# Two transformer layers on one core: layer norms turned by VectorE and transfers, with a token's four chunks side by side

## The chip, the cores and the metric

The kernel runs on one core of a Trainium2 chip. Its engines work side by side and wait for one another through semaphores: TensorE (PE in the profile; PEld is its loading of the stationary operand), VectorE (DVE), ScalarE (ACT), GpSimd (POOL), and SyncE (SP), which issues all of the kernel's transfers between HBM and SBUF. TensorE multiplies a stationary operand (up to 128 x 128) with a moving operand streamed past it, both from SBUF, and writes to PSUM. The metric is the time on the device in microseconds; lower is better. The time of a kernel is the median of its runs; before the change 1811.73 us, of three runs between 1811.0 and 1814.87.

## The reference

Two layers on x of 2 batches x 1024 tokens x 512 features, all in fp32. Each layer norms x over the features and adds a causal attention of 16 heads and a gated feed-forward part, both computed from the same normed x. The first layer's hidden width is 2048, the second's 1408, with scales on gate, up and down.

```python
x = L0_attn_X
xn = _layernorm(x, axis=-1)
x = x + _L0_attn_ref(xn, Wq, Wk, Wv, Wo) + _L0_ffn_ref(xn, w_gate, w_up, w_down)
xn = _layernorm(x, axis=-1)
x = x + _L1_attn_ref(xn, Wq, Wk, Wv, Wo) + _L1_ffn_ref(xn, gate_w, up_w, down_w, gate_s, up_s, down_s)
return x
```

The norm is (x - mean) / sqrt(var + 1e-5). The attention rotates queries and keys by position, masks what lies ahead, takes a softmax over the keys and multiplies with the values and Wo. The feed-forward part is (silu(xn gate^T) * (xn up^T)) down^T.

## The kernel before

The work is cut into four phases, one per layer and batch: (layer 0, batch 0), (0, 1), (1, 0), (1, 1). A phase works on 1024 tokens: eight tiles of 128, or two halves of 512 (`tb`, `TB = 512`). A phase's attention goes in four groups of four heads, each group in four blocks of 256 queries, each block in one to four steps over keys; that makes 40 steps a phase. The softmax of a step runs on ScalarE, VectorE and POOL while TensorE is five steps ahead (`LAG = 5`) with scores.

**xnT.** All projections need the normed x with features on the partitions. It is held as two tiles, `xnT[ph, 0]` and `xnT[ph, 1]`, one per half of the tokens, each of 128 partitions x 4 chunks of features x 512 tokens. The buffers are single: the next phase's tiles take the places of this phase's. For the two halves together, products are formed in a scheme with seven products in place of eight (`class Unit`, line 710, with `first`, `second`, `third` and `fourth`). It also needs differences between the blocks of xnT: the three tiles `xs` (`ln_sums`, line 680) and a last one put in place of a part of `xnT[ph, 1]` (`ln_last_sum`, line 691), all by POOL. `first` reads `xnT[ph, 0]`, `second` reads two of xs, `third` reads `xnT[ph, 1]`, `fourth` the last of xs. `Hidden` units make the hidden layer, `QueriesKeys` units queries and keys; in both xnT and xs are the moving operand of 128 x 512 matmuls (`product`, line 760). `Values` units use xnT and xs as the stationary operand (its own `product`, line 992). Every fp32 matmul leaves two records of TensorE in the profile.

**The norm of a later phase.** Some 22 steps before a phase ends, each tile of the next phase's x is loaded (`load_raw`), and VectorE takes its mean and variance (`ln_stats`); `ln_factors` makes the scale and offset. At the phase's end, when its last unit has read xnT, each tile is loaded once more, scaled by ScalarE (`ln_scale`, line 661), turned by four TensorE transposes of 128 x 128 into a PSUM bank, and copied into xnT by ScalarE (`ln_transpose`, line 668); with the second half come the sums. The products of the last hidden pair with the down weights (`d` in the profile) are done between these tiles. Then `QueriesKeys` of the new phase follows. The first phase has its own form (`ln_pair`, `transpose_pair`).

**What sets the order.** The kernel doesn't emit its instructions as it makes them. `Schedule.record` (line 237) keeps every operation with its dependencies and a cost from a table (`cost`); `emit` and `again` then place all of them on a simulated clock, engine by engine, by the time when they are due for TensorE, and issue them in that order (the call is line 278, so nearly every row of the profile shows that line; rows are told apart by their tiles). SP's queue takes transfers in this order, one after the other, each with its own wait. `class Fill` (line 1416) decides what TensorE does between attention steps: its `main` list holds units and hand-over work in order, `downs` and `outs` hold products that may be pulled forward when the head of `main` would have to wait (`needs` names what an item waits for). `queue_phase` (line 1552) fills these lists for a phase, the hand-over to the next one included.

Of the kernel before, what the change touches and what calls it, by code (L numbers as in the profile page):

```python
# [18 lines left out]
P = 128  # L19
# [3 lines left out]
TB = 512  # L23
# [7 lines left out]
NSQ = QB // SQ  # L31
EPS = 1e-5
# [122 lines left out]
class Schedule:  # L155
# [31 lines left out]
    def cost(self, eng, method, args, kwargs, outs, ins):  # L187
# [6 lines left out]
        if eng is self.tensor:  # L194
            if method == "transpose":
                mode, t = "full", 131.0
            else:
                lhs, rhs = args[1], args[2]
                small_k, small_m = lhs.shape[0] < P, lhs.shape[1] < P
# [306 lines left out]
def two_layers(ctx: ExitStack, tc: tile.TileContext, x_in, attn_w, ffn_w, ffn_s, rope, out):  # L506
# [126 lines left out]
    def transpose_pair(pair):  # L633

        tb, h = divmod(pair, 2)
        if h == 0:
            xnT[0, tb] = xp.tile([P, DC, TB], F32, tag=f"xnT{tb}", name=f"xnT0_{tb}")
        xn = normed.pop((0, pair))
        for n in range(2):
# [3 lines left out]
            (nc.vector.tensor_copy if n else nc.scalar.copy)(xnT[0, tb][:, :, ts(2 * h + n, P)], tr[:, 0])  # L643
# [17 lines left out]
    def ln_scale(ph, t):  # L661
        tb, q = divmod(t, 4)
        rstd, off = stats[ph, tb]
        s = raw_x.pop((ph, t))
        nc.scalar.activation(s, s, AF.Identity, bias=off[:, q : q + 1], scale=rstd[:, q : q + 1])
        normed[ph, t] = s

    def ln_transpose(ph, t):
        tb, q = divmod(t, 4)
        if q == 0:  # L670
            xnT[ph, tb] = xp.tile([P, DC, TB], F32, tag=f"xnT{tb}", name=f"xnT{ph}_{tb}")
        s = normed.pop((ph, t))
        tr = bank(f"tr{ph}_{t}", (P, DC, P))
        for c in range(DC):
            nc.tensor.transpose(tr[:, c, :], s[:, ts(c, P)], ident)
        nc.scalar.copy(xnT[ph, tb][:, :, ts(q, P)], tr)
        if tb == 1:
            ln_sums(ph, q)

    def ln_sums(ph, q):  # L680

        if q == 0:
            xs[ph] = [xp.tile([P, 2, TB], F32, tag=f"xs{n}", name=f"xs{n}_{ph}") for n in (1, 2, 4)]
        t1, t2, t4 = (t[:, :, ts(q, P)] for t in xs[ph])
        b11, b21 = (xnT[ph, 0][:, 2 * c : 2 * c + 2, ts(q, P)] for c in range(2))
        b12, b22 = (xnT[ph, 1][:, 2 * c : 2 * c + 2, ts(q, P)] for c in range(2))
# [4 lines left out]
    def ln_last_sum(ph):  # L691

        for c in range(2):
            b12, b22 = xnT[ph, 1][:, c, :], xnT[ph, 1][:, 2 + c, :]
# [15 lines left out]
    class Unit:  # L710
# [49 lines left out]
        def product(self, bank, a, b, start=False):  # L760
            for c in range(2):
# [3 lines left out]
                    b[:, c, :],  # L765
# [14 lines left out]
        def needs(self, kind):  # L780

            if kind == "second":
# [7 lines left out]
        def first(self):  # L790
# [4 lines left out]
            self.product(self.x, a11, x0[:, 0:2], start=True)  # L795
            one = self.one = keep(self.x, f"p1{self.name}")
            z = bank(f"uz{self.name}")
            self.product(z, a12, x0[:, 2:4], start=True)
# [18 lines left out]
        def third(self, nxt):  # L817
            (_, _, s3, _), _, s4 = self.blocks()
            x1 = xnT[self.ph, 1]
            self.product(self.x, s3, x1[:, 0:2])  # L820
# [3 lines left out]
            self.product(self.y, s4, x1[:, 2:4])  # L824
# [59 lines left out]
    def project_qk(which, tokens):  # L884
# [4 lines left out]
        for c in range(DC):  # L889
            nc.tensor.matmul(  # L890
                ps, wqk[0, 0, which][:, c, :], xnT[0, half][:, c, at : at + n], start=(c == 0), stop=(c == DC - 1)
# [921 lines left out]
```

## Time and profile before

| | |
|---|---|
| median of three runs | 1811.73 us |
| profiled execution, its time | 1814.8 us |
| its span, first to last instruction | 1812.9 us |
| mean granted clock of TensorE | 0.998 |
| PE busy | 1798.0 us, 99% |
| DVE busy | 1476.3 us, 81% |
| POOL busy | 1232.6 us, 68% |
| ACT busy | 1041.7 us, 57% |
| moved by transfers | 165.15 MB, 91 GB/s on average |
| transposes of later phases (tr<-ident,xr) | 96 |
| copies from PSUM into xnT | 28 by ACT, 584 ns each; 4 by DVE, 684 ns each |

Times in a row are microseconds unless marked ns. A row of a group reads: line, engine, operation, written tile <- read tiles, shapes, how many | busy time in all, mean ns of one | idle time of the engine just before them, and what ended it. In a timeline a row reads: start, length, engine, line, operation, how many. Matmuls are pipelined: a record is longer than the distance to the next one's start, so what a matmul costs is read from start to start.

### The profile page before, as it was taken

The page shows a single profiled execution, that of the slowest core. Times are in us where ns is not written, and L with a number is a line of the kernel's source. Part 1 is how long each engine was busy: PE and PEld are TensorE (multiplying, and loading weights), DVE is VectorE, ACT ScalarE, POOL GpSimd, SP SyncE. Part 2 cuts the span into 40 slices and gives each one's busy share as a digit, 9 for nine tenths or more (in the row PEclk, how much of TensorE's full clock was granted, in tenths as well). Part 3 has the DMA queues.
Part 4 walks back from the last instruction along what each step waited for, and adds up shares of the span by engine and source line. Part 5 has one row for each costly group of instructions (what it writes and reads, how often), then busy time and mean ns, then how long its engine had stood idle before and what let it go on. Part 6 is the DMA issues. An engine that isn't in the chain of part 4 may idle for free.

```text
span 1812.9 us, 25807 instructions
## 1 busy us (share of the span) xinstructions
PE 1798.0 (99%) x9406; PEld 880.0 (49%) x9406; DVE 1476.3 (81%) x1975; ACT 1041.7 (57%) x1240; POOL 1232.6 (68%) x1145
## 2 busy tenths in 40 slices
PE   9999999999999999999999999999999999999998
PEld 5464444444444644444444455444444464444443
DVE  3665988868879668779697798888979998989988
ACT  2444665556546565554575556576565757565762
POOL 6726875956868337446377894886779775866775
PEclk9999999999999999999999999999999999999999
DMA  5324343222232422222133324222223322221211
GB/s 192 99 82 137 114 148 120 67 80 82 80 113 88 138 72 68 70 82 89 56 97 102 115 76 160 76 80 71 77 84 98 125 69 71 70 69 50 67 39 71
DMA packets 140334, 165.15 MB, mean 91 GB/s; under 512 B 13360, under 2 KB 93488, under 8 KB 140208
## 3 DMA queue, kind: packets, MB, share of 16 engines
q1 hardware_dynamic: 140208, 163.50, 28.5%
q8 instruction: 75, 1.23, 0.3%
q14 instruction: 51, 0.42, 0.1%
HBM read 134.62 MB, written 28.84 MB: 90 GB/s over the span
## 4 chain that ended last, share of the span: by engine, by line
PE 89%; POOL 5%; DVE 3%; issue 1%; ACT 1%; DMA 1%; SPq 0%; POOLq 0%; ACTq 0%; DVEq 0%
PE d L278 24%; PE ux L278 19%; PE uy L278 9%; PE sc L278 8%; PE av L278 7%; PE ux_qk L278 5%; PE uz L278 5%; POOL acc L278 2%; PE uy_qk L278 2%; PE ux_v L278 2%; PE uz_qk L278 1%; PE uy_v L278 1%; DVE s L278 1%; PE ps_o L278 1%; PE tr L278 1%
## 5 line engine op out<-in xcount | busy, mean ns | idle before, releaser
L278 POOL TENSOR_TENSOR acc<-acc,s 128x512 f32<-128x512 f32 (+1 forms) x378 | 487.4, 1311 | 84.4 <-ACT s L278 79.9
L278 DVE TENSOR_TENSOR s<-s,mb 128x512 f32<-128x512 f32 (+1 forms) x384 | 489.6, 1300 | 12.5 <-DMA mb<-md 12.5
L278 DVE TRANSPOSE_TENSOR_REDUCE rmax<-s 128x32 f32<-128x1024 f32 (+1 forms) x320 | 351.5, 1117 | 63.9 <-POOL s L278 41.3
L278 PE MATMUL d<-wd,hT 128*128 128x512 f32 x864 | 400.1, 593 | 0.0
L278 ACT ACTIVATE s<-s 128x1024 f32<-128x1024 f32 (+1 forms) x320 | 304.9, 970 | 163.0 <-DVE s L278 161.0
L278 ACT ACTIVATE s<-sc 128x1024 f32<-128x1024 f32 (+1 forms) x320 | 283.3, 934 | 195.1 <-PE sc L278 184.0
L278 POOL TENSOR_TENSOR acc<-s 128x512 f32<-128x512 f32 (+1 forms) x128 | 169.2, 1328 | 195.3 <-ACT s L278 191.5
L278 PEld LDWEIGHTS d<-wd,hT 128*128 128x128 f32 x864 | 161.9, 190 | 192.6 <-issue 186.9
L278 ACT ACT_TABLE_LOAD x167 | 214.3, 1283 | 7.7 <-DVE s L278 4.7
L278 DVE TENSOR_TENSOR x<-d,x 128x512 f32<-128x512 f32 x224 | 151.3, 676 | 75.8 <-PE d L278 75.0
L278 PE MATMUL av<-s,v 128*32 128x256 f32 (+1 forms) x2560 | 159.2, 364 | 0.7 <-ACT s L278 0.5
L278 POOL TENSOR_SCALAR_AFFINE_SELECT s<-s 128x512 f32<-128x512 f32 x128 | 98.9, 784 | 67.0 <-ACT s L278 65.0
L278 PEld LDWEIGHTS av<-s,v 128*32 128x32 f32 x2560 | 67.6, 109 | 145.7 <-issue 97.2
L278 POOL TENSOR_TENSOR hT<-p,hT 128x512 f32<-128x512 f32 x53 | 72.5, 1367 | 77.9 <-ACT hT L278 77.9
L278 PE MATMUL d<-wo,oT 128*128 128x512 f32 x198 | 103.0, 602 | 1.2 <-DVE hT L278 1.2
L278 PE MATMUL ux<-xs,ws 128*128 128x512 f32 x212 | 101.7, 602 | 0.6 <-ACT p L278 0.6
L278 PE MATMUL ux<-xnT,wu 128*128 128x512 f32 x212 | 101.8, 602 | 0.1
L278 PE MATMUL ux<-xnT,wg 128*128 128x512 f32 x212 | 100.9, 598 | 0.4 <-DVE hT L278 0.4
L278 PE MATMUL ux<-xs,wu 128*128 128x512 f32 x212 | 101.2, 600 | 0.0
L278 PE MATMUL uy<-xs,ws 128*128 128x512 f32 x212 | 99.7, 593 | 0.3 <-DVE hT L278 0.3
L278 PE MATMUL uy<-xnT,ws 128*128 128x512 f32 x212 | 99.8, 593 | 0.0
L278 PE MATMUL uz<-xnT,wg 128*128 128x512 f32 x212 | 99.7, 593 | 0.0
(179 smaller groups left out, 2511.2 us busy)
## 6 DMA issues: line engine op xcount, KB each, us to landing
mb<-md SPq DMA_DIRECT2D x64, 512.0 KB, 3.8
wg<-in_gate SPq DMA_DIRECT2D x54, 256.0 KB, 2.9
wd<-in_down SPq DMA_DIRECT2D x32, 256.0 KB, 2.9
xr<-xm SPq DMA_DIRECT2D x32, 256.0 KB, 2.7
wu<-in_up SPq DMA_DIRECT2D x28, 256.0 KB, 3.0
s12gu<-ws SPq DMA_DIRECT2D x26, 256.0 KB, 2.0
ws<-s12gu SPq DMA_DIRECT2D x26, 256.0 KB, 2.6
wd<-wds SPq DMA_DIRECT2D x22, 256.0 KB, 2.9
```

What stands on the lines that cost most here:

```text
L278: target(*[get(a) for a in args], **{k: get(a) for k, a in kwargs.items()})
```

## The change

In the three later phases TensorE no longer transposes. Earlier in the phase before, when the factors are there, each tile is loaded again and scaled by ScalarE, and VectorE turns it in blocks of 32 x 32 into a tile `turned_x` in which a token's four feature chunks lie side by side. Four transfers per tile write it to HBM, which puts the blocks of a chunk on their partitions (runs of 512 bytes). When the last unit of the phase has read an old half of xnT, four transfers read the new half in (2 KB for each partition and tile). POOL makes all the sums after both halves are there. Statistics and scaling start some steps earlier, and `first` is told to wait for `xnT[ph, 0]`.

The layout of xnT and xs changes everywhere, the first phase included: from chunk x token to token x chunk. A chunk's tokens are then 16 bytes apart in xnT and 8 bytes apart in xs, where they were adjacent. All matmuls that read them, POOL's sums, and the first phase's copies out of PSUM follow.

```diff
     def transpose_pair(pair):
...
-            xnT[0, tb] = xp.tile([P, DC, TB], F32, tag=f"xnT{tb}", name=f"xnT0_{tb}")
+            xnT[0, tb] = xp.tile([P, TB, DC], F32, tag=f"xnT{tb}", name=f"xnT0_{tb}")
...
-            (nc.vector.tensor_copy if n else nc.scalar.copy)(xnT[0, tb][:, :, ts(2 * h + n, P)], tr[:, 0])
+            (nc.vector.tensor_copy if n else nc.scalar.copy)(
+                xnT[0, tb][:, ts(2 * h + n, P)], tr[:, 0].rearrange("p c t -> p t c")
+            )
...
     def ln_scale(ph, t):
...
         nc.scalar.activation(s, s, AF.Identity, bias=off[:, q : q + 1], scale=rstd[:, q : q + 1])
-        normed[ph, t] = s
-
-    def ln_transpose(ph, t):
-        tb, q = divmod(t, 4)
+        turned_x = tmp.tile([P, QSQ, SQ, DC], F32, tag="swapped", name=f"xt{ph}_{t}")
+        nc.vector.transpose(turned_x.rearrange("p f s c -> p c f s"), s.rearrange("p (c f s) -> p c f s", f=QSQ, s=SQ))
+        to = normed[ph, t] = xd.tile([P, QSQ, P], F32, tag=f"xn{t}", name=f"xnd{ph}_{t}")
+        for a in range(QSQ):
+            nc.sync.dma_start(
+                out=to[:, a, :].rearrange("(f s) e -> s f e", s=SQ),
+                in_=turned_x[ts(a, SQ)].rearrange("p f s c -> p f (s c)"),
+            )
+
+    def ln_read(ph, tb):
+        xnT[ph, tb] = xp.tile([P, TB, DC], F32, tag=f"xnT{tb}", name=f"xnT{ph}_{tb}")
+        for q in range(4):
+            nc.sync.dma_start(
+                out=xnT[ph, tb][:, ts(q, P)].rearrange("p t c -> p (t c)"), in_=normed.pop((ph, 4 * tb + q)).rearrange("p a e -> p (a e)")
+            )
...
-        if q == 0:
-            xnT[ph, tb] = xp.tile([P, DC, TB], F32, tag=f"xnT{tb}", name=f"xnT{ph}_{tb}")
-        s = normed.pop((ph, t))
-        tr = bank(f"tr{ph}_{t}", (P, DC, P))
-        for c in range(DC):
-            nc.tensor.transpose(tr[:, c, :], s[:, ts(c, P)], ident)
-        nc.scalar.copy(xnT[ph, tb][:, :, ts(q, P)], tr)
-        if tb == 1:
-            ln_sums(ph, q)
...
+            xs[ph] = [xp.tile([P, TB, 2], F32, tag=f"xs{n}", name=f"xs{n}_{ph}") for n in (1, 2, 4)]
+        t1, t2, t4 = (t[:, ts(q, P)] for t in xs[ph])
+        b11, b21 = (xnT[ph, 0][:, ts(q, P), 2 * c : 2 * c + 2] for c in range(2))
+        b12, b22 = (xnT[ph, 1][:, ts(q, P), 2 * c : 2 * c + 2] for c in range(2))
...
         def product(self, bank, a, b, start=False):
...
-                    b[:, c, :],
+                    b[:, :, c],
...
         def needs(self, kind):
+            if kind == "first":
+                return [xnT[self.ph, 0]]
...
     class Values(Unit):
...
-                        b[:, c, ts(2 * self.pair + n, P)],
+                        b[:, ts(2 * self.pair + n, P), c],
...
     def queue_phase(ph):
...
-                fill.at(t0 + per_phase - 22 + t, lambda t=t: load_raw(nxt, t))
-                fill.at(t0 + per_phase - 21 + t, lambda t=t: ln_stats(nxt, t))
-            fill.at(t0 + per_phase - 12, lambda: ln_factors(nxt, range(2)))
+                fill.at(t0 + per_phase - 24 + t // 2, lambda t=t: load_raw(nxt, t))
+                fill.at(t0 + per_phase - 23 + t // 2, lambda t=t: ln_stats(nxt, t))
+            fill.at(t0 + per_phase - 19, lambda: ln_factors(nxt, range(2)))
+            for t in range(QC):
+                fill.at(t0 + per_phase - 19 + t, lambda t=t: load_raw(nxt, t))
+                fill.at(t0 + per_phase - 18 + t, lambda t=t: ln_scale(nxt, t))
...
-        fill.main.insert(len(fill.main) - 2, (0.0, lambda: (raw(0), raw(1)), "other", None, 0))
-        fill.main.insert(len(fill.main) - 1, (0.0, lambda: scale(0), "other", None, 0))
-        for t in range(QC):
-
-            def one(t=t):
-                ln_transpose(nxt, t)
-                raw(t + 2)
-                scale(t + 1)
-
-            fill.add(0.7, one, "other", lambda t=t: [normed[nxt, t]])
-            if t == 1:
-                fill.add(0.0, waits)
-        fill.add(0.0, lambda: (ln_last_sum(nxt), marks.append(nxt)))
+        fill.main.insert(len(fill.main) - 3, (0.0, lambda: ln_read(nxt, 0), "other", None, 0))
+        fill.main.insert(len(fill.main) - 1, (0.0, lambda: ln_read(nxt, 1), "other", None, 0))
+        fill.add(0.0, waits)
+
+        def sums():
+            for q in range(4):
+                ln_sums(nxt, q)
+            ln_last_sum(nxt)
+            marks.append(nxt)
+
+        fill.add(0.0, sums)
```

The matmuls of `first`, `third`, `project_qk` and `hidden` follow the new layout in the same way, and the schedule's cost table now takes all of a stationary operand's columns to tell a small matmul from a full one.

## The prediction

> **What bounds the kernel now.** I read the page first for the engines' shares, then the timeline of TensorE around the first hand-over between phases, then the groups of instructions by shape.
>
> ```profile
> span 1812.9 us, 25807 instructions
> ...
> PE 1798.0 (99%) x9406; PEld 880.0 (49%) x9406; DVE 1476.3 (81%) x1975; ACT 1041.7 (57%) x1240; POOL 1232.6 (68%) x1145
> ...
> PE   9999999999999999999999999999999999999998
> ...
> PE 89%; POOL 5%; DVE 3%; issue 1%; ACT 1%; DMA 1%; SPq 0%; POOLq 0%; ACTq 0%; DVEq 0%
> ```
>
> TensorE (PE) works in every slice and is 89% of the chain that ended last. No other engine is full. So an edit is worth what it takes from, or adds to, TensorE's own list of work, as long as the other engines keep up. The hand-over itself, in the timeline (start, length, instruction, how many):
>
> ```profile
> 458.02 0.66 PE L278 MATMUL tr<-ident,xr 128*128 128x128 f32 x4
> 458.51 1.88 PE L278 MATMUL d<-wd,hT 128*128 128x512 f32 x4
> ...
> 480.30 0.60 PE L278 MATMUL tr<-ident,xr 128*128 128x128 f32 x4
> 480.74 3.60 PE L278 MATMUL d<-wd,hT 128*128 128x512 f32 x8
> 484.18 0.60 PE L278 MATMUL tr<-ident,xr 128*128 128x128 f32 x4
> 484.61 1.88 PE L278 MATMUL ux_qk<-xnT,wq 128*128 128x512 f32 x4
> 486.33 1.88 PE L278 MATMUL uz_qk<-xnT,wq 128*128 128x512 f32 x4
> ```
>
> Read start to start: a group of four transposes costs 0.43 to 0.50 us, and four records of 512 columns cost 1.72 us (484.61 to 486.33). That is 0.43 us a record, 0.84 ns a column, and it is the same wherever I looked. Each fp32 matmul of the program leaves two records. There is no idle time at this hand-over, so the transposes cost only their own length.
>
> **The change, part by part.** The sum is made against the profiled execution: 1814.8 us, of which 1812.9 is the span and 1.9 lies around it. It is 3.1 us above the median of the runs, 1811.73.
>
> *Transposes removed.* The eight groups of the first hand-over take 3.68 us start to start (0.49, 0.95 for two, 0.50, 0.44, 0.43, 0.44, 0.43). Three hand-overs: **-11.0 us** of TensorE's time. ScalarE also loses 24 copies out of PSUM at 0.58 us each; at 57% busy that buys nothing.
>
> *The new layout under the matmuls.* This is the part that nobody's list of instructions shows. In the changed kernel a chunk of xnT is read with 16 bytes from one token to the next; before, tokens were adjacent. Counted in the changed kernel's own order of instructions: 568 matmuls of 512 columns stream xnT, and 16 of 256 columns. Times two records: 1136 and 32, or 1152 records of full length. The xs tiles are read with a step of 8 bytes in 408 more (816 records). No row before has TensorE reading with a step, so the cost is bounded. From below: nothing. From above, by the nearest row, VectorE reading fp32 from SBUF with a wide step:
>
> ```profile
> L278 DVE TRANSPOSE_TENSOR_REDUCE rmax<-s 128x32 f32<-128x1024 f32 x192 | 232.8, 1224 | 22.4 <-ACT s L278 21.8
> L278 DVE TRANSPOSE_TENSOR_REDUCE rmax<-s 128x24 f32<-128x768 f32 x128 | 118.7, 955 | 41.5 <-POOL s L278 41.3
> L278 DVE TENSOR_REDUCE m<-mtr 32x32 f32<-32x128 f32 x64 | 17.2, 269 | 18.6 <-PE mtr L278 17.9
> L278 DVE TENSOR_REDUCE m<-rmax 128x32 f32<-128x256 f32 x16 | 9.3, 580 | 0.3
> L278 DVE TENSOR_REDUCE m<-rmax 128x32 f32<-128x128 f32 x16 | 5.8, 360 | 0.3
> ```
>
> Adjacent elements: (1224 - 955) / 256 = 1.05 ns each. With a step of 64 bytes (m from rmax): (580 - 360) / 128 = 1.72 ns. A step in PSUM (m from mtr) costs nothing of the kind, 269 ns for 128. So a read that meets a new piece of SBUF at every element pays, and the price is 1.72 ns. The Trainium skill, page "SBUF — State Buffer", section "Door 1: The DMA port swizzle", speaks against the change: SBUF is read in lines of 16 bytes, and a line must be hit at least twice for full speed. With 16 bytes from token to token each line is hit once, with 8 bytes twice. (The same passage also calls a stride of four fp32 free, so it does not decide alone; no run so far shows TensorE under it.)
>
> What each gives: by the row in absolute time, 512 x 1.72 = 0.88 us a record, 1152 x 0.45 = +519 us. By the row's ratio, 1.72 / 1.05 = 1.64, 1152 x 0.43 x 0.64 = +317 us. By the rule, read as one line taking the time of two elements, twice 0.43, 1152 x 0.43 = **+495 us**. I take the last: it lies between the two readings of the row and close to the absolute one (2 x 0.84 = 1.68 ns against 1.72), which I trust more than the ratio because VectorE's and TensorE's own steps differ. For xs I take nothing, as two elements share a line.
>
> *Stationary reads.* For the values, xnT and xs are the stationary operand: 448 loads of 128 columns, beside streams of 256 columns that take 0.215 us each. A load's record is 190 ns. If the 256 of them that load from xnT double their 128 x 0.84 = 107 ns, they just reach the end of their cover: between 0 and 256 x 0.107 = 27 us; I take **+10**.
>
> *VectorE's transposes.* 24 of 128x512. The row of the existing block transpose is 445 ns for 256; with 256 more at 1.05 ns it is 0.71 us, with stepped writes at 1.72 up to 1.15 us. That is 17 to 28 us in all, spread over some 20 of a phase's 40 steps; VectorE was busy 45.2 of the 58 us before the hand-over. TensorE runs five steps behind the softmax that VectorE feeds, and that covers it: **0**; uncovered, it is the 17 to 28 us.
>
> *Transfers.* Per phase 32 writes and 8 reads join SP's queue, 120 in all, at about 0.32 us of queue each (the issues of md and xr take that): 38 us of SP in 1800, and 12.6 MB on top of 165. What is moved past SP's queue: a write waits for its transpose, and behind it stand the weights and the pair md, mb of the row maxima, for which VectorE's subtraction waits (12.5 us in the whole run now). A write late by 2 us makes a subtraction late by 2 us, within the same five steps: **0**, at most +20.
>
> *The new wait at the hand-over.* The first product of the new phase waits for four reads of xnT, the second for eight differences that POOL makes after all eight reads. Summing TensorE's own work in the new order, from the last read of the old second half: 17.5, 19.2 and 21.1 us until the new phase's first product, and 29.9, 31.6 and 27.6 us until its first use of xs. A 256 KB read lands in 2.7 us, four of them in about 6. Eight differences took 0.73 us each, 6 us; with half as much again for steps over 8 bytes (the Trainium skill, "GPSIMD Engine Reference", section "Performance pitfalls for Q7 kernels"; no row here has such a step) 9 us. 6 + 9 = 15 against 27.6 leaves some 12 us for POOL's other work in between: **0**. Without that cover, each late microsecond is one on the end. The last sums, two of 1.39 us per phase, are needed later still.
>
> *The first phase.* The eight copies into xnT now read PSUM with a step (m from mtr: no price) and write 16-byte pieces: **0**, at most +3. Statistics and scaling only move earlier.
>
> Sum: 1814.8 - 11.0 + 495 + 10 = 2308.8 in a profiled run; less 3.1, **2305 us**.
>
> **The rivals.**
>
> *The step is free for TensorE (the other side).* In the av groups four 32-column matmuls stream side by side: 16 records of 256 columns in 1.00 us, four times the words of one stream out of the same partitions. So SBUF can give TensorE a word per 0.21 ns; if one fp32 stream, which uses only one per 0.84 ns, can draw on that, nothing is lost. Against it: those are four streams, each on its own adjacent line. Then 1814.8 - 11.0 - 3.1 = 1800.7, with a little for the first phase about **1802 us**. The sign turns at 11.0 / 1152 = 9.5 ns a record, 2.2% of 0.43 us: below that the change gains, above it loses.
>
> *A part of the price.* If VectorE's ratio carries over, +317: **2128 us**; contention of the many lines with the other engines' reads alone could be anything from +10 up.
>
> *The step is free, but the hand-over is late.* POOL or a transfer overruns its 12 us of cover by more than 5 us at each of three places, which outweighs the 11: **1815 to 1835 us**. The cover speaks against it.
>
> *No change that can be measured:* gain and small losses meet, 1808 to 1815 us.
>
> **How the numbers follow.** Full doubling 0.42, free 0.33, part of the price 0.13, late hand-over 0.07, no change 0.05. Within 0.2%, 3.6 us, a measurement of this kernel can't tell from no change. So faster 0.33, same 0.05, slower 0.62. The likeliest case's own range is 2270 to 2335 us (the row's absolute price on top, a few ns less a record below). Since both signs hold much of the chance, the range reaches from 1798 to 2335: it leaves out a gain beyond the transposes, and a doubling that also takes the stationary loads or the xs tiles at full price, together about 0.1.
>
> **What would show it.** Doubling: four records of a product on xnT stand 3.4 us apart, start to start, those on xs still 1.72; PE stays at 99%, while the shares of VectorE, ScalarE and POOL fall by a fifth. Free: both stay at 1.72 and the transposes are simply gone. Late hand-over: idle time of PE before ux_qk, released by a DMA or by POOL's xs. I am wrong outright if TensorE buffers whole lines or reads each word twice from one line, so that the step never shows.

## The result

The changed kernel takes **2358.1 us** (median of four runs, 2356.9 to 2358.6), beside 1812.7 us for the kernel before (1811.0 to 1814.9). The ratio is **1.301 [1.299, 1.303]**: 545 us slower. The prediction was 2305 us, with a range up to 2335. Direction and mechanism are those of the likeliest case; the size is 53 us short, a tenth of the loss, and the time lies 23 us above the range. Each ratio further on is against runs of the kernel before that were made beside that experiment (medians from 1811.3 to 1811.8 us).

The profile page of the kernel after, with the span, the engines' busy time, the chain that ended last, and four groups (busy us, mean ns of one record):

```profile
span 2356.8 us, 25763 instructions
...
PE 2345.2 (100%) x9310; PEld 900.2 (38%) x9310; DVE 1439.0 (61%) x1996; ACT 1038.6 (44%) x1219; POOL 1195.0 (51%) x1146
...
PE 98%; DVE 1%; POOL 1%; DMA 0%; issue 0%; ACT 0%; SPq 0%; POOLq 0%; DVEq 0%; ACTq 0%
...
L279 PE MATMUL d<-wd,hT 128*128 128x512 f32 x864 | 399.9, 594 | 0.0
...
L279 PE MATMUL ux<-xnT,wu 128*128 128x512 f32 x212 | 201.0, 1082 | 0.0
...
L279 PE MATMUL ux<-xs,wu 128*128 128x512 f32 x212 | 106.4, 623 | 0.0
```

TensorE runs 96 records fewer (the transposes' own) and is busy 547 us longer. The other engines do about the same microseconds of work as before in a span that is 30% longer, so their shares fall by a quarter: VectorE from 81% to 61%, ScalarE from 57% to 44%, POOL from 68% to 51%. Products that never touch xnT (`d`) have the length they had. Those on xnT have nearly doubled, and those on xs are a little longer than `d`. The same groups in the kernel before (busy us, mean ns) show that all three were alike:

```profile
L278 PE MATMUL d<-wd,hT 128*128 128x512 f32 x864 | 400.1, 593 | 0.0
...
L278 PE MATMUL ux<-xnT,wu 128*128 128x512 f32 x212 | 101.8, 602 | 0.1
...
L278 PE MATMUL ux<-xs,wu 128*128 128x512 f32 x212 | 101.2, 600 | 0.0
```

The timeline of TensorE at a hand-over of the kernel after (start, length, instruction, how many):

```profile
636.90 3.70 PE L279 MATMUL d<-wd,hT 128*128 128x512 f32 x8
640.44 3.76 PE L279 MATMUL ux_qk<-xnT,wq 128*128 128x512 f32 x4
644.02 3.78 PE L279 MATMUL uz_qk<-xnT,wq 128*128 128x512 f32 x4
647.62 1.90 PE L279 MATMUL d<-wd,hT 128*128 128x512 f32 x4
...
656.76 1.96 PE L279 MATMUL ux_qk<-xs,ws_qk 128*128 128x512 f32 x4
658.56 1.96 PE L279 MATMUL uy_qk<-xs,ws_qk 128*128 128x512 f32 x4
660.36 1.88 PE L279 MATMUL d<-wd,hT 128*128 128x512 f32 x4
```

Start to start, four records on xnT take 3.58 to 3.60 us (640.44 to 644.02 to 647.62), or 0.90 us each; before it was 0.43. Four records on xs take 1.80 us, or 0.45 each. No bracket with an idle time stands in these lines: the new phase starts without a wait, and the transposes are gone from between the `d` products. The other two hand-overs, at 1286 and 1796 us, show no wait either. All of the loss is in the length of matmuls.

### The profile page after: what moved, and what is told of

Same layout as the page of the kernel before. It is cut to its first block, busy times and chain, and to the rows that moved or that the text cites. A ratio compares the mean times of both kernels' runs of the same rounds, so it can differ in the third digit from the quotient of the medians.

```text
span 2356.8 us, 25763 instructions
## 1 busy us (share of the span) xinstructions
PE 2345.2 (100%) x9310; PEld 900.2 (38%) x9310; DVE 1439.0 (61%) x1996; ACT 1038.6 (44%) x1219; POOL 1195.0 (51%) x1146
## 4 chain that ended last, share of the span: by engine, by line
PE 98%; DVE 1%; POOL 1%; DMA 0%; issue 0%; ACT 0%; SPq 0%; POOLq 0%; DVEq 0%; ACTq 0%
PE ux L279 25%; PE d L279 19%; PE uy L279 12%; PE uz L279 8%; PE ux_qk L279 7%; PE sc L279 7%; PE av L279 6%; PE uy_qk L279 3%; PE ux_v L279 3%; PE uz_qk L279 2%; PE uy_v L279 1%; PE ps_o L279 1%; POOL acc L279 1%; PE uz_v L279 1%; PE ps_k L279 1%; PE g L279 1%
## 5 line engine op out<-in xcount | busy, mean ns | idle before, releaser
L279 POOL TENSOR_TENSOR acc<-acc,s 128x512 f32<-128x512 f32 (+1 forms) x379 | 465.0, 1246 | 168.0 <-ACT s L279 151.0
L279 DVE TENSOR_TENSOR s<-s,mb 128x512 f32<-128x512 f32 (+1 forms) x384 | 433.5, 1153 | 5.6 <-DMA mb<-md 5.5
L279 ACT ACT_TABLE_LOAD x170 | 218.1, 1283 | 14.6 <-DVE s L279 11.6
L279 PE MATMUL ux<-xnT,wu 128*128 128x512 f32 x212 | 201.0, 1082 | 0.0
L279 PE MATMUL uz<-xnT,wg 128*128 128x512 f32 x212 | 200.3, 1079 | 0.0
L279 PE MATMUL uy<-xnT,ws 128*128 128x512 f32 x212 | 200.3, 1078 | 0.0
L279 PE MATMUL ux<-xnT,wg 128*128 128x512 f32 x212 | 200.1, 1078 | 0.0
L279 POOL TENSOR_SCALAR_AFFINE_SELECT s<-s 128x512 f32<-128x512 f32 x128 | 88.0, 696 | 139.3 <-ACT s L279 136.7
L279 DVE TENSOR_TENSOR hT<-uz,p 128x512 f32<-128x512 f32 x53 | 36.7, 692 | 198.5 <-PE uz L279 177.5
L279 ACT ACTIVATE hT<-hT 128x512 f32<-128x512 f32 x62 | 39.1, 630 | 203.4 <-DVE hT L279 203.3
L279 PE MATMUL ux<-xs,wu 128*128 128x512 f32 x212 | 106.4, 623 | 0.0
```

Source lines behind the costliest of these rows:

```text
L279: target(*[get(a) for a in args], **{k: get(a) for k, a in kwargs.items()})
```

## The experiments

The theory, from the prediction: the step of 16 bytes makes TensorE's own reads slow, each new 16-byte piece costs a fixed time, and everything else in the change costs nothing. Rivals: the added turning and the transfers cost something themselves, or the many reads collide with those of other engines. A second question came up on the way: where do the 11 us go that the removed transposes should have given?

### steps: TensorE alone, one step after another

A small kernel with one stationary operand and a moving operand of 512 columns, each pattern in 16 matmuls (32 records in fp32, 16 in bf16).

```diff
+    def stepped(t, k, n=N):
+        return t[:, 0:n] if k == 1 else t[:, 0 : n * k].rearrange("p (n k) -> p n k", k=k)[:, :, 0]
...
+    for name, k in STEPS.items():
+        product(name, w, stepped(data, k), N)
+    product("pairs", w, data[:, 0 : 2 * N].rearrange("p (n k) -> p n k", k=4)[:, :, 0:2], N)
+    product("runs", w, data[:, 0 : 4 * N].rearrange("p (n k) -> p n k", k=128)[:, :, 0:32], N)
```

> This kernel leaves the layers out: it only copies x to the output and measures single instructions on data in SBUF, with no other engine's work to compete. 16 fp32 matmuls of 512 columns (32 records) for each step between the words of the moving operand. Theory A (a price per line of 16 bytes, met by TensorE alone): records 0.43 us apart at steps of 4 and 8 bytes, 0.88 to 0.90 at 16, and no more than that at 32 and 64 bytes; at 12 bytes, where three of four words meet a new line, about 0.67; two adjacent words out of four (one line per two words) 0.43. Rival B (any step other than adjacent costs, or the price grows with the distance): 8 bytes already well above 0.43, or 64 bytes well above 16. Rival C (the slow records of the changed kernel come from the other engines' traffic in SBUF, not from the step): 0.43 at every step here. In bf16, where TensorE takes a word in half the time, A expects the price at the same 16 bytes, as 8 words. Loads of 128 columns: A expects 107 ns each beside adjacent words, 215 to 225 ns at 16 bytes. VectorE's copies: 1.05 ns a word adjacent, 1.7 ns at 16 and at 64 bytes.

Its timeline on TensorE (start, length, instruction, how many):

```profile
39.95 13.90 PE L44 MATMUL adjacent<-data,w 128*128 128x512 f32 x32
53.69 14.56 PE L44 MATMUL two<-data,w 128*128 128x512 f32 x32
68.09 21.81 PE L44 MATMUL three<-data,w 128*128 128x512 f32 x32
89.73 28.97 PE L44 MATMUL four<-data,w 128*128 128x512 f32 x32
118.52 29.30 PE L44 MATMUL five<-data,w 128*128 128x512 f32 x32
147.64 28.77 PE L44 MATMUL six<-data,w 128*128 128x512 f32 x32
176.24 29.55 PE L44 MATMUL eight<-data,w 128*128 128x512 f32 x32
205.60 27.63 PE L44 MATMUL sixteen<-data,w 128*128 128x512 f32 x32
233.06 14.58 PE L44 MATMUL pairs<-data,w 128*128 128x512 f32 x32
247.48 13.89 PE L44 MATMUL runs<-data,w 128*128 128x512 f32 x32
261.21 3.62 PE L44 MATMUL half_adjacent<-half,whalf 128*128 128x512 bf16 x16
264.66 3.77 PE L44 MATMUL half_two<-half,whalf 128*128 128x512 bf16 x16
268.28 7.38 PE L44 MATMUL half_four<-half,whalf 128*128 128x512 bf16 x16
275.48 14.58 PE L44 MATMUL half_eight<-half,whalf 128*128 128x512 bf16 x16
289.88 14.87 PE L44 MATMUL half_sixteen<-half,whalf 128*128 128x512 bf16 x16
```

From start to next start (304.57 us for the last), divided by the number of records:

| pattern | 16-byte pieces met in 512 columns | us a record | pieces x 1.76 ns |
|---|---|---|---|
| fp32 adjacent, or 32 of 128 | 128 | 0.429 | 0.225 |
| fp32, 8 bytes; two adjacent of four | 256 | 0.450 | 0.451 |
| fp32, 12 bytes | 384 | 0.676 | 0.676 |
| fp32, 16 bytes | 512 | 0.900 | 0.901 |
| fp32, 20 bytes | 512 | 0.910 | 0.901 |
| fp32, 24 bytes | 512 | 0.894 | 0.901 |
| fp32, 32 bytes | 512 | 0.918 | 0.901 |
| fp32, 64 bytes | 512 | 0.858 | 0.901 |
| bf16 adjacent | 64 | 0.216 | 0.113 |
| bf16, 4 bytes | 128 | 0.226 | 0.225 |
| bf16, 8 bytes | 256 | 0.450 | 0.451 |
| bf16, 16 bytes | 512 | 0.900 | 0.901 |
| bf16, 32 bytes | 512 | 0.918 | 0.901 |

One rule fits to 2%, except that a step of 64 bytes is 5% cheaper: a record takes the longer of its own time and **1.76 ns for every new 16-byte piece**. The 1.76 is itself 0.900 / 512, so the other rows are the test of it. My expectation for bf16, that only a step of 16 bytes pays, was a miss: 8 bytes already double it. The rule explains that: bf16's own time is half of fp32's, while the piece costs the same. Fp32 at 8 bytes lies 5% over its own time, so two words a piece are not quite free.

The price does not follow TensorE's clock either. In the row of bf16 at 16 bytes the granted clock fell to half (PEclk, the eighth column, after the busy times of the five engines):

```profile
275.50:277.80 2.30, 2.30 (x4) 0.34 (x3) 0.00 (x0) 0.00 (x0) 0.00 (x0) 1.00 0.00 0
278.00:289.80 11.80, 11.80 (x14) 1.61 (x13) 0.00 (x0) 0.00 (x0) 0.00 (x0) 0.50 0.00 0
```

Its records stood 0.900 us apart before and after, and 32 bytes took 0.918 us in fp32 at a clock of 1.00 and in bf16 at 0.50. TensorE had not stopped before this fall; what caused it was not tested.

The stationary operand was tried beside streams of 64 columns. A load of 128 adjacent columns and its stream took 0.209 us, one with a step of 16 bytes 0.233 (expected for the load: 107 ns adjacent, 215 to 225 at 16 bytes). The granted clock was 0.50 in all of this part, and twice 107 ns is 214, so the adjacent number is no price at full clock, and the two can't be compared; the second is near 128 x 1.76 = 225 ns.

### layout_alone: the new layout, nothing else

TensorE's transposes, their places and all transfers are those of the kernel before.

```diff
-            xnT[ph, tb] = xp.tile([P, DC, TB], F32, tag=f"xnT{tb}", name=f"xnT{ph}_{tb}")
+            xnT[ph, tb] = xp.tile([P, TB, DC], F32, tag=f"xnT{tb}", name=f"xnT{ph}_{tb}")
...
-        nc.scalar.copy(xnT[ph, tb][:, :, ts(q, P)], tr)
+        nc.scalar.copy(xnT[ph, tb][:, ts(q, P)], tr.rearrange("p c t -> p t c"))
...
-            xs[ph] = [xp.tile([P, 2, TB], F32, tag=f"xs{n}", name=f"xs{n}_{ph}") for n in (1, 2, 4)]
+            xs[ph] = [xp.tile([P, TB, 2], F32, tag=f"xs{n}", name=f"xs{n}_{ph}") for n in (1, 2, 4)]
...
-                    b[:, c, :],
+                    b[:, :, c],
...
```

> The kernel before with nothing but the new layout of xnT and xs: TensorE still transposes. Theory A: the changed kernel's time plus the transposes, 2358 + 11 = 2369 us (2362 to 2376). Rival B (the other half of the change brings the loss): near 1812 us.

Measured: 2366.2 us, ratio 1.306 [1.304, 1.308], as expected. Its groups of TensorE (busy us, mean ns) are those of the kernel after:

```profile
L278 PE MATMUL ux<-xnT,wu 128*128 128x512 f32 x212 | 201.0, 1082 | 0.0
...
L278 PE MATMUL ux<-xs,wu 128*128 128x512 f32 x212 | 106.0, 621 | 0.0
```

The layout alone makes the whole loss. The span is 2363.9 us, 7 us over that of the kernel after (the medians are 8 apart): that is what the transposes still cost here. Their 11 us of records are gone from the kernel after, but TensorE idles 2 us more there (11.6 us of its span against 9.5), and its granted clock was 0.97 over the first 50 us against 1.00 here, which is 1.5 us by estimate.

### old_layout: everything else, the layout undone

VectorE turns, the tiles travel through HBM, but xnT and xs keep a chunk's tokens adjacent. The reads then land in runs of 128 bytes.

```diff
-        turned_x = tmp.tile([P, QSQ, SQ, DC], F32, tag="swapped", name=f"xt{ph}_{t}")
+        turned_x = tmp.tile([P, QSQ, DC, SQ], F32, tag="swapped", name=f"xt{ph}_{t}")
...
-        xnT[ph, tb] = xp.tile([P, TB, DC], F32, tag=f"xnT{tb}", name=f"xnT{ph}_{tb}")
-        for q in range(4):
+        xnT[ph, tb] = xp.tile([P, DC, TB], F32, tag=f"xnT{tb}", name=f"xnT{ph}_{tb}")
+        turned = normed.pop((ph, tb))
+        for c in range(DC):
             nc.sync.dma_start(
-                out=xnT[ph, tb][:, ts(q, P)].rearrange("p t c -> p (t c)"), in_=normed.pop((ph, 4 * tb + q)).rearrange("p a e -> p (a e)")
+                out=xnT[ph, tb][:, c, :].rearrange("p (b s) -> p b s", s=SQ), in_=turned[:, :, ts(c, SQ)]
             )
...
```

> The change without its second half: VectorE turns the tiles and transfers carry them as in the changed kernel, but xnT and xs keep the old layout, chunk by token, adjacent (the reads from HBM then land in runs of 128 bytes). Theory A (the step under TensorE is the whole loss): all of it comes back and the transposes are saved, 1812 - 11 = 1801 us, at worst 1806 with the small transfers. Rival B (transfers, VectorE's load or the hand-over cost a good part): 1830 us or more, with idle time of TensorE ahead of the first products of queries and keys.

Measured: 1813.7 us (1810.1 to 1817.2), ratio 1.0013 [1.0005, 1.0020]. All but 2 us of the loss is gone. With layout_alone this rules out that the turning or the transfers make it, and `steps`, where no other engine works beside TensorE, rules out a collision with others. But the 1801 to 1806 us of the expectation were missed: the removed transposes give nothing here. The profile shows a place where time is lost. First SP's queue around the first hand-over (start, length, instruction, how many):

```profile
438.78 5.42 SPq L279 DMA_DIRECT2D xnT<-xnd  x4
444.24 2.01 SPq L279 DMA_DIRECT2D wg<-in_gate  x1
446.36 0.44 SPq L279 DMA_DIRECT2D md<-m  x1
450.74 0.33 SPq L279 DMA_DIRECT2D mb<-md  x1
```

Four reads in runs of 128 bytes hold the queue for 5.42 us, 1.35 each. Behind them stands the pair md, mb. TensorE then stops (in brackets its idle time and what ended it):

```profile
459.26 1.67 PE L279 MATMUL d<-wo,oT 128*128 128x512 f32 x2 [2.21 <-DVE hT L279]
460.72 3.08 PE L279 MATMUL d<-wd,hT 128*128 128x512 f32 x4
463.64 0.59 PE L279 MATMUL d<-wo,oT 128*128 128x512 f32 x1
```

The stop is 2.21 us, and after it four records take 2.92 us (460.72 to 463.64) instead of 1.72. The granted clock (PEclk, the eighth column) is half for 3.4 us after the stop, then 1.00 again:

```profile
457.00:459.50 2.50, 0.29 (x2) 0.24 (x2) 2.50 (x4) 1.49 (x2) 1.24 (x2) 1.00 0.96 150
459.70:463.10 3.40, 3.40 (x5) 1.35 (x4) 3.02 (x5) 0.28 (x1) 2.24 (x3) 0.50 0.75 130
```

The second hand-over has such a stop too, 1.87 us at 951.47, but there the clock stayed at 1.00.

### pairs: two chunks side by side

Every step is 8 bytes: each chunk shares its pieces with one other. Turning, writes, reads, sums and products follow.

```diff
-            xnT[0, tb] = xp.tile([P, TB, DC], F32, tag=f"xnT{tb}", name=f"xnT0_{tb}")
+            xnT[0, tb] = xp.tile([P, 2, TB, 2], F32, tag=f"xnT{tb}", name=f"xnT0_{tb}")
...
```

> The changed kernel with two chunks side by side in place of four: xnT is read with a step of 8 bytes, like xs. If a line of 16 bytes must be hit twice (theory A): records on xnT 0.45 us apart like those on xs in the changed kernel, 1812 - 11 + 1968 records x 0.02 = 1840 us. If the price goes with the step as such (rival): half-way, some 2080 us.

Measured: 1844.0 us, ratio 1.018 [1.017, 1.020], as expected by the theory. In its timeline of TensorE (start, length, instruction, how many) four records on xnT take 1.80 us, not 1.72:

```profile
70.11 1.96 PE L279 MATMUL ux<-xnT,wg 128*128 128x512 f32 x4
71.91 1.96 PE L279 MATMUL uz<-xnT,wg 128*128 128x512 f32 x4
73.71 1.88 PE L279 MATMUL d<-wd,hT 128*128 128x512 f32 x4
```

So the size of the step decides, and the remaining 0.02 us a record are worth 1968 x 0.02 = 39 us (30 measured against old_layout, 36.5 in TensorE's busy time). Even this form is 1.8% slower than before.

### engines: the same steps on the other engines

A small kernel that copies 512 words and reduces 256 or 64, on one engine after the other.

```diff
+    for engine in (nc.vector, nc.scalar, nc.gpsimd):
+        copy = engine.copy if engine is nc.scalar else engine.tensor_copy
+        for name in plan:
+            for i in range(4):
+                copy(sb.tile([P, N], F32, tag="to", name=f"from_{name}"), stepped(data, STEPS[name]))
```

> This kernel leaves the layers out: it copies x to the output and runs single copies and reductions on one engine after another, with nothing beside them. It asks whether the row that the prediction took its price from, VectorE's reduction at 1.72 ns a word, was a price for new lines at all. Theory A (VectorE pays per line as TensorE does, 1.76 ns): a reduction of 256 adjacent words takes some 330 ns against 580 at a step of 64 bytes, and a copy of 512 words at 16 bytes some 0.95 us. Rival (the 1.72 ns belong to that reduction, and its nearness to TensorE's 1.76 is luck): the reduction takes 580 ns with adjacent words too, and the copy at 16 bytes stays near 0.6 us. ScalarE: 0.62 us for 512 adjacent words, 1.13 us at 16 bytes, 0.9 us at 12. POOL: more at 16 bytes than at 8.

Groups by shape (busy us, mean ns of one | idle before it, and what ended it); `four` is a step of 16 bytes:

```profile
L48 DVE TENSOR_REDUCE summany_four<-data 128x32 f32<-128x256 f32 x4 | 2.5, 620 | 0.1
L48 DVE TENSOR_REDUCE summany_adjacent<-data 128x32 f32<-128x256 f32 x4 | 1.7, 420 | 0.1
L48 DVE TENSOR_REDUCE sumfew_four<-data 128x32 f32<-128x64 f32 x4 | 1.1, 269 | 0.1
L48 DVE TENSOR_REDUCE sumfew_adjacent<-data 128x32 f32<-128x64 f32 x4 | 0.9, 218 | 0.1
L37 ACT COPY from_four<-data 128x512 f32<-128x512 f32 x4 | 4.5, 1130 | 0.1
L37 POOL COPY from_four<-data 128x512 f32<-128x512 f32 x4 | 4.4, 1092 | 0.2
```

VectorE's reduction takes (420 - 218) / 192 = 1.05 ns a word adjacent and (620 - 269) / 192 = 1.83 at 16 bytes; at 64 bytes (592 against 262) it is 1.72. That is the 1.72 which the prediction read from the row of `m` from `rmax`. So the row was a fair price, though it showed the slightly cheaper 64 bytes. ScalarE needs 618, 663, 884 and 1130 ns for 4, 8, 12 and 16 bytes, POOL 612, 646, 866 and 1092. From 12 to 16 bytes there are 128 pieces more, or 1.9 and 1.8 ns each. VectorE's copies pay less: 427, 427, 500, 614 ns, 0.9 ns a piece over the same stretch. The expectations were met in part: a reduction does pay for pieces, but the adjacent one took 420 ns, not 330; and the copy at 16 bytes took the 0.6 us of the rival, not 0.95, so VectorE's operations don't have one price.

### small_writes, told, staged: where did the 11 us go?

Three forms of old_layout. In `small_writes` the small pieces come earlier, in 16 writes for each tile, and the reads have runs of 512 bytes:

```diff
+        to = normed[ph, t] = xd.tile([P, DC, P], F32, tag=f"xn{t}", name=f"xnd{ph}_{t}")
         for a in range(QSQ):
-            nc.sync.dma_start(
-                out=normed[ph, tb][:, QSQ * q + a, :].rearrange("(f s) e -> s f e", s=SQ),
-                in_=turned_x[ts(a, SQ)].rearrange("p f c s -> p f (c s)"),
-            )
+            for c in range(DC):
+                nc.sync.dma_start(
+                    out=to[:, c, ts(a, SQ)].rearrange("(f s) e -> s f e", s=SQ), in_=turned_x[ts(a, SQ), :, c, :]
+                )
...
+        for q in range(4):
+            nc.sync.dma_start(out=xnT[ph, tb][:, :, ts(q, P)], in_=normed.pop((ph, 4 * tb + q)))
```

> The kernel with the old layout and VectorE's turning once more, but the pieces of 128 bytes are now made by the writes, spread over the steps before the hand-over (16 writes a tile in place of 4), and the reads at the hand-over land in runs of 512 bytes. Theory (the 11 us that the missing transposes freed were lost because four reads of small pieces hold SP's queue for 5.4 us, and the row maxima behind them come late to VectorE and so to TensorE): the gain comes through, 1801 to 1806 us. Rival (VectorE's 17 us of turning, or the lack of transposes as filler, took them): still 1811 to 1815 us.

Measured: 1819.3 us, ratio 1.0042 [1.0030, 1.0054], slower than either expectation: a miss for both. 384 writes stand in SP's queue in place of 96, and VectorE's waits for mb sum to 18.2 us (20.0 in old_layout).

In `told` the order's cost table learns what the reads cost SP:

```diff
             size = 4 * int(np.prod((outs or ins)[0].shape, dtype=int))
+            if outs and outs[0].tile.tag.startswith("xnT"):
+                return 1350.0, 5500.0
```

> The kernel with the old layout and reads in pieces of 128 bytes, but the schedule's table is told what such a read costs SP's queue (1.35 us in place of 0.45), so that the exchange of the row maxima is put between the four reads. If SP's queue, held by these reads, is what ate the transposes' 11 us at the hand-overs, a part comes back: 1806 to 1811 us. If the pieces also fill the transfer engines behind the queue, or if it is VectorE's extra work, nothing does: 1812 to 1816 us.

Measured: 1821.5 us, ratio 1.0056 [1.0042, 1.0070]: both expectations missed again. The waits for mb do fall, to 12.0 us, but the new order has TensorE wait for ScalarE and VectorE at the third hand-over instead (stops of 3.59, 2.60 and 2.14 us between 1360 and 1394 us), and the granted clock was 0.86 from 1350 to 1400 us, where it is 1.00 in the kernel before: 7 us by estimate.

In `staged` no transfer has short runs: reads of 2 KB land in a staging tile, and ScalarE copies into place (24 copies of 615 ns, about what it did out of PSUM before).

```diff
...
-        for c in range(DC):
+        for q in range(4):
+            staged = tmp.tile([P, QSQ, DC, SQ], F32, tag="xs", name=f"xg{ph}_{4 * tb + q}")
             nc.sync.dma_start(
-                out=xnT[ph, tb][:, c, :].rearrange("p (b s) -> p b s", s=SQ), in_=turned[:, :, ts(c, SQ)]
+                out=staged.rearrange("p a c s -> p (a c s)"), in_=normed.pop((ph, 4 * tb + q)).rearrange("p a e -> p (a e)")
+            )
+            nc.scalar.copy(
+                xnT[ph, tb][:, :, ts(q, P)].rearrange("p c (a s) -> p c a s", s=SQ),
+                staged.rearrange("p a c s -> p c a s"),
             )
```

> The same without small pieces anywhere: writes of 512 bytes as in the changed kernel, reads of 2 KB into a staging tile, and ScalarE copies each tile from there into the old layout, in runs of 32 adjacent words (24 copies at some 0.62 us, as many as it made out of PSUM before). SP's queue then carries what the changed kernel's carries. Theory (small pieces ate the gain): 1801 to 1806 us. Rival (VectorE's turning or the missing filler ate it): 1811 us or more.

Measured: 1811.9 us, ratio 1.0002 [0.9994, 1.0010]. The rival holds: with short runs the time was some 2 us longer (1.0013 against 1.0002), not 11. The form has costs of its own, though: 24 copies on ScalarE, and a staging tile that shares two buffers with other loads (tag `xs`).

### unturned and turned_twice: does VectorE's turning cost anything?

`staged` once without VectorE's transposes, once with each of them done twice.

```diff
...
-        nc.vector.transpose(turned_x.rearrange("p f c s -> p c f s"), s.rearrange("p (c f s) -> p c f s", f=QSQ, s=SQ))
...
-                in_=turned_x[ts(a, SQ)].rearrange("p f c s -> p f (c s)"),
+                in_=s[ts(a, SQ)].rearrange("p (f e) -> p f e", f=QSQ),
```

> The staged kernel without VectorE's 24 transposes: the scaled tiles are written to HBM as they are, so the later phases work on features in the wrong places. All other instructions and transfers stay. If VectorE's 17 us of turning (24 x 0.69) are what eats the 11 us that TensorE's transposes gave back, the gain appears: 1800 to 1806 us. If it is the missing filler at the hand-overs or the order of the softmax work, which stay: 1809 to 1814 us.

> The staged kernel with each of VectorE's transposes done twice into the same tile: 17 us more of VectorE, nothing else. If VectorE's time decides: 1816 to 1829 us (a third of it to all of it). If not: 1810 to 1814 us, as staged.

Measured: 1812.5 us, ratio 1.0005 [0.9996, 1.0013], without; 1810.9 us, ratio 0.9991 [0.9984, 0.9998], doubled. Neither moves by what 24 transposes of 0.69 us are (17 us). In this form VectorE's turning is covered, as the prediction had it.

### left_out: the transposes taken away, nothing put in their place

The kernel before, in whose later phases ScalarE copies the scaled tile straight into xnT.

```diff
-        tr = bank(f"tr{ph}_{t}", (P, DC, P))
-        for c in range(DC):
-            nc.tensor.transpose(tr[:, c, :], s[:, ts(c, P)], ident)
-        nc.scalar.copy(xnT[ph, tb][:, :, ts(q, P)], tr)
+        nc.scalar.copy(xnT[ph, tb][:, :, ts(q, P)], s.rearrange("p (c t) -> p c t", c=DC))
```

> The kernel before with the 96 transposes of the later phases left out and nothing in their place: ScalarE copies the scaled tile straight into xnT, so the later phases work on features in the wrong places. It gives the most that the removal can bring. If TensorE's own list sets the end, as the prediction had it: 1811.5 - 11 = 1800 to 1802 us. If the softmax chains set the pace around the hand-overs, so that time taken from TensorE there comes back as waiting: 1806 us or more, with less PE busy and more idle time ahead of av, d and the hidden products.

Measured: 1805.4 us, ratio 0.9968 [0.9956, 0.9980]. It lies between the two expectations: the removal gives 5.8 us, by the interval 3.6 to 8.0, and not 11. In its timeline TensorE stops in new places (in brackets):

```profile
1400.91 1.13 PE L278 MATMUL av<-s,v 128*32 128x256 f32 x16 [2.02 <-DVE oT L278]
...
1407.66 0.62 PE L278 MATMUL av<-s,v 128*32 128x256 f32 x4 [1.31 <-ACT s L278]
```

When the transposes go, TensorE runs into its softmax sooner, and a part of their time comes back: as waits (17.8 us of idle time in its span, 14.9 in the kernel before) and as a lower clock behind them. After the stop of 2.02 us the granted clock (eighth column) was half for 3.4 us:

```profile
1401.80:1405.20 3.40, 3.40 (x22) 2.06 (x19) 3.40 (x4) 1.90 (x3) 2.06 (x2) 0.50 0.03 5
```

Over the six runs the granted clock averages 0.998, over those of the kernel before beside them 1.000. That is 0.002 x 1805 = 3.6 us by estimate, and with 3 us more of idle time some 6 us, about what is missing (5 us). The division is not measured: the two profiled runs alone lie 10.3 us apart, since that of the kernel before (1814.8 us) had itself a clock of 0.93 over its first 50 us.

`staged` gives back the other 6 us too. It runs the same 9310 records on TensorE, but these are busy 1790.0 us in place of 1784.4, and the idle time of its span is 20.2 us in place of 17.8. Its timeline shows how:

```profile
385.32 3.57 PE L279 MATMUL ux<-xs,wu 128*128 128x512 f32 x4 [1.77 <-DVE p L279]
388.69 2.03 PE L279 MATMUL ux<-xnT,wg 128*128 128x512 f32 x4
```

A stop of 1.77 us, and the four records after it take 3.37 us in place of 1.72, again at a granted clock of 0.50. What makes the stops of this form is not settled. It isn't VectorE's turning, and short runs are about 2 us. The order of the softmax's work and of SP's transfers is left, and in `staged` the shared buffers; no run here isolates them. Nor was a layout tried that keeps runs of 32 tokens of a chunk together in xnT and so needs neither a short-run read nor a copy: `runs` in the first experiment says that TensorE would stream it at 0.429 us; whether the stationary reads of the values would allow it is open.

## Where the prediction was right, and the step that failed

The path and the mechanism held. The step that failed is the price of a 16-byte piece in the term of the layout, taken too low for xnT and at nothing for xs.

*What bounds the kernel.* Right: TensorE was the end before (89% of the chain) and is more so after (98%), so an addition to its own list of work is paid in full.

*The layout under the matmuls: the step that failed, by its size.* The mechanism was the named one, and the count of 1152 records held. The price did not:

| term | taken | measured |
|---|---|---|
| xnT as moving operand, 1152 records | 0.43 us each, +495 | 0.895 - 0.43 = 0.465 each, +536 |
| xs as moving operand, 816 records | nothing | 0.45 - 0.43 = 0.02 each, +16 |
| stationary reads, 32 groups of eight records | +10 | 0.14 us a group, +4 |
| transposes removed | -11.0 | all 96 records gone, -11 |
| idle time of TensorE (span less busy) | 0 | 14.9 to 11.6, -3 |
| VectorE's turning, transfers, new wait | 0 | 0 at every hand-over |
| sum | +494 | +542, against 544 between the two spans |

The prediction was 53 us short. Two choices made 57 us. The smaller term of the loads and the idle time take back 9; the 3.1 us that were subtracted for the median add 3, since the profiled run of after (2358.6) is hardly slower than its median; 2 are left over.

First, between the row (1.72 ns a word) and the rule read as twice TensorE's own 0.84, I took the rule, since it lay between two readings. The true price is 1.76 ns: the row's absolute time and a little more, because the row showed a step of 64 bytes, the cheaper one (0.858 against 0.900 us on TensorE). That is 41 us. A fixed time for a piece is not a multiple of the reader's own pace, and the ratio, which would have given 317 us, was the wrong way to carry it. That "twice" came so near is luck of fp32: in bf16 the same piece takes four times TensorE's own time (0.900 against 0.216 us). Second, "two elements share a line" was taken as nothing; a piece of two words takes 1.76 ns where TensorE's own time for two columns is 1.68, and 816 records make 16 us of it.

The range ended at 2335 because its top was the row's price (+519, a sum of some 2330) with xs still at nothing. What lies above that sum is the rest of the price of xnT (17 us) and xs (16), less what the loads and the idle time gave back.

On the Trainium skill's page "SBUF — State Buffer", section "Door 1: The DMA port swizzle": its line of 16 bytes is what the runs show. Its "at least twice" is close for fp32 (0.450 against 0.429 us) and fails for bf16, where two words of a line make 0.450 against 0.216; its free stride of four fp32 fails outright (0.900). The measurements decide.

*Stationary reads.* The mechanism held: they just pass their cover. The groups by shape, first before, then after (busy us, mean ns of a load):

```profile
L278 PEld LDWEIGHTS ux_v<-wv,xnT 128*128 128x128 f32 x128 | 23.8, 190 | 5.7 <-issue 1.6 <-ACT s L278 0.5 <-DVE x L278 0.3
```

```profile
L279 PEld LDWEIGHTS ux_v<-wv,xnT 128*128 128x128 f32 x128 | 31.4, 326 | 2.7 <-issue 1.1 <-DVE x L279 0.3 <-DVE rec L279 0.3
```

By the rule of the first experiment, which was tested there for the moving operand alone, a load needs 128 x 1.76 = 225 ns, beside a stream of 215. Eight records that load from xnT take 1.86 us where they took 1.72.

*Transposes removed.* "There is no idle time at this hand-over, so the transposes cost only their own length" is right for their records: all 11 us of them are gone from TensorE's list. It is not right for the end of the kernel. In the old layout a shorter hand-over meets the softmax earlier, and only 6 us stay (3.6 to 8.0 by the interval); idle time and the clock behind it take the rest, as far as `left_out` shows. Against layout_alone, where the other engines have time to spare, 7 to 8 us stay.

*VectorE's transposes: 0.* Right. They take 1.09 us each with stepped writes, inside the 0.71 to 1.15 that were given (0.69 with adjacent writes in old_layout). With adjacent writes, doubling or dropping them in `staged` changes nothing.

*Transfers and the new wait: 0.* Right for the changed kernel. Writes land in 2.0 us and reads in 3.5; the four that were put at 6 us did not delay TensorE anywhere; VectorE's waits for mb fell from 12.5 to 5.5 us. Part of that cover is the loss itself, which gives every other engine more time. In old_layout, where the reads have short runs and TensorE is fast, the very wait that the prediction named (md and mb behind the reads on SP's queue) appears: 20.0 us of VectorE's, and a stop of TensorE.

*POOL's sums.* Put at half as much again for steps; they took a median of 748 and 847 ns in place of 727 and 728. They read two adjacent words of each piece. The last sums, which do read with 16 bytes, took a median of 1153 ns in place of 1275, so no price of the step shows in them, though POOL's plain copies at 16 bytes took 78% more in `engines` (1092 against 612 ns). Why is not shown.

*What would show it.* Four records on xnT at 3.4 us: 3.58. Those on xs "still 1.72": 1.80. Shares down by a fifth: by a quarter. The rivals: the free step is excluded by `steps` (its argument had a slip: 16 records of 256 columns in 1.00 us are 0.24 ns a word, not 0.21); the part price was VectorE's ratio, which does not carry; no late hand-over appears.

## What to carry to other kernels

Before a layout is turned for a transfer's sake, count the 16-byte pieces of SBUF that the busiest engine will meet per instruction, and compare 1.76 ns a piece with that engine's own time; carry the price over as absolute time, not as a ratio. An operand that is streamed hundreds of times should have its inner dimension adjacent, even if the one write of it becomes dearer: here 96 transposes were worth 6 to 8 us and the layout 550. And where an estimate has terms set to nothing, the range needs their upper ends on top of that of the main term.

## What the runs showed beyond that

- The price of a piece is nearly the same for TensorE in fp32 and bf16 (1.76 ns), copies on ScalarE (1.9) and POOL (1.8), and VectorE's reductions (1.83); VectorE's copies pay about half. On TensorE it was the same at a granted clock of 1.00 and of 0.50. A step of 64 bytes is 4 to 7% cheaper than one of 16 on every engine.
- At a step of 8 bytes fp32 products lose 5%, bf16 products double (0.216 to 0.450 us).
- A read of 256 KB in runs of 128 bytes holds SP's queue for 1.35 us and lands in 5.5 us; in the changed kernel, with 2 KB runs, it lands in 3.5.
- Stops of TensorE of 1.77, 2.02 and 2.21 us (`staged`, `left_out`, `old_layout`) were each followed by some 3.4 us at a granted clock of 0.50, where four 512-column records took 2.92 and 3.37 us in place of 1.72: with that such a stop costs one and a half times to twice its own length, by estimate. One of 1.87 us in `old_layout` was not. So the same work of TensorE in other orders ended between 1805 and 1821 us, with 17.8 to 27.5 us of idle time and mean granted clocks from 0.994 to 0.998; how much each of the two makes is not separated.
